# Halves at the ends of layers 2 and 3, and four column groups for two small products, in a four-layer graph network

## The chip, the cores and the metric

The kernel runs on one core of a Trainium2 chip. The metric is the device time of one launch in microseconds (us), from the first to the last instruction of the program. A core has a matrix engine (TensorE, "PE" in the profile, with "PEld" for its loads of the stationary operand), a vector engine (VectorE, "DVE"), a scalar engine (ScalarE, "ACT"), GpSimd ("POOL") and a queue engine that issues transfers (SyncE, "SP"). Each engine works through its own list of instructions in order and waits for the others by semaphores.

## The reference, cut to what matters

Sixteen graphs of 1024 nodes with 128 features pass through four layers. Each layer's output is added to its input and then normalised over the features.

```python
# x [16,1024,128], adj [16,1024,1024]
x = _layernorm(x + L0(x, adj))             # attention with one gate
x = _layernorm(x + L1(x, adj, nodemask))   # dilated adjacency, three SAGE steps, batch norm
x = _layernorm(x + L2(x, adj))             # attention with three gates
x = _layernorm(x + L3(x, adj))             # two graph convolutions

def _sage(x, adj, Wr, Wx, b, mf):          # three times in layer 1, with the dilated adj
    deg = jnp.clip(jnp.sum(adj, axis=-1, keepdims=True), 1.0, None)
    agg = jnp.einsum('bij,bjd->bid', adj, x) / deg
    out = agg @ Wr + x @ Wx + b
    ...

# the end of layer 2, with h_prime the attention's result
concat = jnp.concatenate([x, h_prime], axis=-1)
i_c = sigmoid(einsum('bnc,oc->bno', concat, ig_w) + ig_b)   # one number per node
f_c = sigmoid(einsum('bnc,oc->bno', concat, fg_w) + fg_b)
o_c = sigmoid(einsum('bnc,oc->bno', concat, og_w) + og_b)
h_joint = sigmoid(i_c * h_prime + f_c * x)
return o_c * tanh(h_joint)
```

## The kernel before

Sizes in the code: `P = 128`, `N = 1024`, `NT = N // P = 8`, `H2 = 2`, `B = 16`. The program runs layer 0, the dilation of the adjacency, the three steps of layer 1, and then layers 2 and 3 together. A layer's work on one batch is a generator, and `take_turns` lets several of them issue a stretch each in turn, so that the work of neighbouring batches lies side by side in the engines' lists.

Helpers. `halves` hands out a PSUM tile of 512 columns for each half of a batch, `turned` transposes a batch through it, `gates` (already used by layer 0) is the packed product that the change uses once more, and `normed` is a layer norm.

```python
    def gates(psum, out, *pairs):
        p = psum.tile([P, N // 4], F32, name="pq", tag="h")
        for i, (g, x) in enumerate(pairs):
            for q in range(4):
                nc.tensor.matmul(p[32 * q:32 * q + 32, :], g, x[:, q * N // 4:(q + 1) * N // 4], start=(i == 0),
                                 stop=(i == len(pairs) - 1), tile_position=(0, 32 * q))
        nc.scalar.copy(out, p)
        p = psum.tile([P, 2, P], F32, name="pg", tag="h")
        for t in range(2):
            nc.tensor.transpose(p[:, t, :], out[:, t * P:(t + 1) * P], identf)
        return p.rearrange("p t (q g) -> p q t g", q=4)

    def normed(small, r):
        st = small.tile([P, NT, 6], F32, name="ln_st")
        mv = small.tile([P, NT, 2], F32, name="ln_mv")
        for i in range(NT):
            nc.vector.bn_stats(st[:, i, :], r[:, i, :])
        for i in range(NT):
            nc.vector.bn_aggr(mv[:, i, :], st[:, i, :])
        rstd = power_mhalf(small, mv[:, :, 1], add=LN_EPS, name="ln_rstd")   # the power is on GpSimd
        nb = small.tile([P, NT], F32, name="ln_nb")
        nc.vector.scalar_tensor_tensor(nb, mv[:, :, 0], -1.0, rstd, op0=OP.mult, op1=OP.mult)
        for i in range(NT):
            nc.scalar.activation(r[:, i, :], r[:, i, :], AF.Identity, scale=rstd[:, i:i + 1], bias=nb[:, i:i + 1])
```

Layer 1, first step. `degree_product` multiplies the adjacency by a stationary block of twos, so that each of the 128 output rows holds the same row of degrees; the row then goes through memory to be turned and inverted.

```python
        def degree_product(A):
            for h in range(H2):
                c = slice(h * 512, (h + 1) * 512)
                acc = ps_a.tile([P, 512], F32, name="acc")
                for jt in range(NT):
                    nc.tensor.matmul(acc, twos[:, :P], A[:, jt, c], start=(jt == 0), stop=(jt == NT - 1))   # L1261
                yield acc, c
            # ... cut ...
            def first(self, b):
                st = self.batches[b]
                row = work.tile([1, N], F16, name="row", bufs=1)
                for acc, c in degree_product(st.A):
                    nc.scalar.copy(row[:, c], acc[0:1, :])                     # L1357
                d16 = small.tile([NT, P], F16, name="d16", bufs=1)
                nc.gpsimd.dma_start(d16, row)
                nc.vector.tensor_reduce(nodeg[:NT, b:b + 1], d16, AX.X, OP.min)  # L1360
                # ... cut: halve, clip, invert, store and load it as a broadcast tile rdeg ...
                # ... cut: transposes of x, the adjacency product, times rdeg ...
            def out(self, b):
                # ... cut: o = x @ Wx + ag @ Wr + b, by halves in PSUM tiles of the same pool ...
                for h, sq in enumerate(banks):
                    k = slice(4 * h, 4 * h + 4)
                    nc.scalar.activation(sq, o[:, k, :], AF.Square)
                    nc.vector.tensor_reduce(ss[:, k], sq, AX.X, OP.add)        # L1397
```

Layers 2 and 3. `before` makes layer 1's output, adds it to x, normalises and makes the attention's operands; `attention` is the eight-part attention; `after` has the gates, the mix, layer 2's norm, layer 3 and its norm.

```python
        def before(s, b):
            # ... cut: yT = layer 1's last product ...
            for p, c, k in turned(ps_h, yT):
                nc.vector.tensor_mul(yn[:, k, :], tiles3(p), half_rows(mf[:, b * NT + k.start:b * NT + k.stop]))
            nc.vector.tensor_add(s.xn, s.xn, yn)
            yield
            normed(small, s.xn)
            # ... cut: transposes of xn, hT, G, hn ...

        def after(s, b):
            hpT = wide("hpT")
            nc.scalar.activation(hpT, s.acc, AF.Relu)
            pg = ps_h.tile([P, NT, 3], F32, name="pg", tag="h")
            for i in range(NT):
                c = slice(i * P, (i + 1) * P)
                nc.tensor.matmul(pg[:, i, :], s.xT[:, c], gw[:, 0, :], start=True, stop=False)   # L1600
                nc.tensor.matmul(pg[:, i, :], hpT[:, c], gw[:, 1, :], start=False, stop=True)    # L1601
            # ... cut: bias, tanh, scale -> gt [P, NT, 3] ...
            for p, c, k in turned(ps_h, hpT):
                nc.vector.tensor_mul(yn[:, k, :], tiles3(p), half_rows(gt[:, k, 0]))
            f = rows("x3T")
            nc.vector.tensor_mul(f, s.xn, per_row(gt[:, :, 1]))
            nc.vector.tensor_add(yn, yn, f)
            nc.scalar.activation(yn, yn, AF.Tanh, scale=0.5)
            nc.scalar.activation(yn, yn, AF.Tanh, scale=0.5, bias=half)
            nc.vector.tensor_mul(yn, yn, per_row(gt[:, :, 2]))
            nc.vector.tensor_add(s.xn, s.xn, yn)
            yield
            normed(small, s.xn)
            # ... cut: layer 3 ...
            normed(small, s.xn)
            nc.gpsimd.dma_start(nat(out[b]), s.xn)
```

Of the kernel before, what the change touches and what calls it, by code (L numbers as in the profile page):

```python
# [9 lines left out]
F32 = mybir.dt.float32  # L10
# [629 lines left out]
def fast_kernel(ctx: ExitStack, tc: tile.TileContext, t: dict, out: bass.AP, flag: bass.AP):  # L640
# [142 lines left out]

        return v[:, :, None].to_broadcast([P, 4, P])

    def normed(small, r):

        st = small.tile([P, NT, 6], F32, name="ln_st")
        mv = small.tile([P, NT, 2], F32, name="ln_mv")
        for i in range(NT):  # L790
            nc.vector.bn_stats(st[:, i, :], r[:, i, :])  # L791
        for i in range(NT):
            nc.vector.bn_aggr(mv[:, i, :], st[:, i, :])
        rstd = power_mhalf(small, mv[:, :, 1], add=LN_EPS, name="ln_rstd")
        nb = small.tile([P, NT], F32, name="ln_nb")
        nc.vector.scalar_tensor_tensor(nb, mv[:, :, 0], -1.0, rstd, op0=OP.mult, op1=OP.mult)  # L796
        for i in range(NT):
            nc.scalar.activation(r[:, i, :], r[:, i, :], AF.Identity, scale=rstd[:, i:i + 1], bias=nb[:, i:i + 1])  # L798

    class Batch:  # L800
        pass
# [381 lines left out]
    class Layers23:  # L1183
# [53 lines left out]
    with ExitStack() as ph:  # L1237
# [16 lines left out]

        def degree_product(A):

            for h in range(H2):
                c = slice(h * 512, (h + 1) * 512)
                acc = ps_a.tile([P, 512], F32, name="acc")
                for jt in range(NT):  # L1260
                    nc.tensor.matmul(acc, twos[:, :P], A[:, jt, c], start=(jt == 0), stop=(jt == NT - 1))  # L1261
                yield acc, c

        def widened(A):

# [22 lines left out]
        class Step:  # L1288
# [63 lines left out]
            def first(self, b):  # L1352
# [7 lines left out]
                nc.vector.tensor_reduce(nodeg[:NT, b:b + 1], d16, AX.X, OP.min)  # L1360
# [116 lines left out]
    with ExitStack() as ph:  # L1477
# [54 lines left out]
        def before(s, b):  # L1532
# [60 lines left out]
        def after(s, b):  # L1593

            hpT = wide("hpT")
            nc.scalar.activation(hpT, s.acc, AF.Relu)
            pg = ps_h.tile([P, NT, 3], F32, name="pg", tag="h")
            for i in range(NT):
                c = slice(i * P, (i + 1) * P)
                nc.tensor.matmul(pg[:, i, :], s.xT[:, c], gw[:, 0, :], start=True, stop=False)  # L1600
                nc.tensor.matmul(pg[:, i, :], hpT[:, c], gw[:, 1, :], start=False, stop=True)  # L1601
            gt = small.tile([P, NT, 3], F32, name="gt")
            nc.vector.tensor_add(gt, pg, gb[:, None, :].to_broadcast([P, NT, 3]))
# [6 lines left out]
            nc.vector.tensor_mul(f, s.xn, per_row(gt[:, :, 1]))  # L1610
            nc.vector.tensor_add(yn, yn, f)
            nc.scalar.activation(yn, yn, AF.Tanh, scale=0.5)
            nc.scalar.activation(yn, yn, AF.Tanh, scale=0.5, bias=half)
            nc.vector.tensor_mul(yn, yn, per_row(gt[:, :, 2]))
            nc.vector.tensor_add(s.xn, s.xn, yn)
# [92 lines left out]
```

## Time and profile before

The median of three runs is 3050.43 us (3050.39 to 3054.73). Times below are from the profiled run, whose span is 3049.5 us and whose mean granted TensorE clock is 0.966.

| stretch, us from the start | what runs | length | PE busy | granted clock |
|---|---|---|---|---|
| 1145 to 1525 | layer 1, first step | 380.0 | 369.8 | 1.00 |
| 1780 to 1872 | end of layer 1, layers 2 and 3 begin | 92.0 | 64.7 | 0.88 |
| 1872 to 1957 | first batches of layers 2 and 3 | 85.0 | 82.0 | 0.93 |
| 1957 to 2936 | layers 2 and 3, batches side by side | 979.0 | 956.3 | 0.95 |
| 2936 to 3049.5 | the last two batches end | 113.5 | 78.3 | 0.84 |

A row of such a table is read from the view of busy time by stretch: PE busy is the time in which at least one matrix product was open, and the granted clock is the mean share of full speed that the throttle let through. Products overlap in the records, so the step from one start to the next, and not the length of a record, is what one of them costs. The profile page puts 58% of the chain that ended last on PE, and in its row of 40 slices (76 us each) PE stands at 9 in every slice from 1144 us on but three: the two from 1753 to 1906 us, where layer 1 gives way to layers 2 and 3, and the last one.

### The profile page before, as it was taken

How to read it: one execution, taken by the hardware profiler on the slowest of the kernel's cores; microseconds unless marked ns; L12 is line 12 of the kernel's file. 1: busy time of each engine (PE TensorE's matmuls, PEld its weight loads, DVE VectorE, ACT ScalarE, POOL GpSimd, SP SyncE). 2: the span in 40 equal slices, each digit the busy share in tenths (PEclk: the TensorE clock that was granted, in tenths of full speed). 3: DMA queues.
4: the chain of work that ended last, by engine and by line, in shares of the span. 5: the costliest groups of instructions: out<-in, count | busy, mean ns of one | idle time of the engine just before them, and what ended most of it. 6: DMA issues, size and time to landing. Idle time of an engine off the chain costs nothing.

```text
span 3049.5 us, 42855 instructions
## 1 busy us (share of the span) xinstructions
PE 2825.3 (93%) x15187; PEld 1794.2 (59%) x15250; DVE 2325.2 (76%) x5972; ACT 2018.8 (66%) x3425; POOL 315.2 (10%) x292
## 2 busy tenths in 40 slices
PE   7999999996999989999999987999999999999995
PEld 3444444443666657777788873556555555555554
DVE  7898889887999986666678785676766776777665
ACT  5877787773888886655555435666666666666653
POOL 0000000003000001111122231000000000000000
PEclk9999999997999999999999998999999999999997
DMA  5344344430000043223367692011112211111000
GB/s 162 131 159 152 132 138 159 152 118 29 2 2 2 2 158 107 88 91 120 122 231 251 227 336 76 35 63 59 66 57 71 73 57 56 56 56 56 21 14 22
DMA packets 123217, 297.97 MB, mean 98 GB/s; under 512 B 12656, under 2 KB 64624, under 8 KB 115824
## 3 DMA queue, kind: packets, MB, share of 16 engines
q1 hardware_dynamic: 102384, 211.13, 20.6%
q0 software_dynamic: 20608, 84.00, 7.7%
q8 instruction: 122, 2.00, 0.3%
q14 instruction: 103, 0.84, 0.1%
HBM read 211.04 MB, written 84.02 MB: 97 GB/s over the span
## 4 chain that ended last, share of the span: by engine, by line
PE 58%; DVE 21%; ACT 9%; DMA 5%; issue 5%; POOL 3%; SPq 0%; POOLq 0%; ACTq 0%; DVEq 0%
PE acc L1284 9%; PE pmm L723 8%; PE ph L1527 7%; PE acc L1590 6%; PE ph L765 6%; PE ph L758 4%; PE ph L1388 4%; DMA an<-in_adj 3%; ACT xn L798 3%; PE s L1131 2%; PE acc L969 2%; POOL ln_rstd L744 2%; PE ph L1513 2%; DVE mid L1085 2%; DVE ln_st L791 2%
## 5 line engine op out<-in xcount | busy, mean ns | idle before, releaser
L723 PE MATMUL pmm<-G,hT 128*128 128x512 f32 x1024 | 520.2, 630 | 1.9 <-DVE mx L1576 1.4
L723 PEld LDWEIGHTS pmm<-G,hT 128*128 128x128 f32 x1024 | 188.3, 201 | 174.2 <-issue 148.7
L798 ACT ACTIVATE xn<-xn,ln_nb,ln_rstd 128x128 f32<-128x128 f32 x512 | 206.6, 481 | 91.9 <-DVE ln_nb L796 91.9
L1590 PE MATMUL acc<-em,hs 128*128 128x512 f32 x512 | 256.0, 612 | 12.1 <-DVE hs L1587 10.5
L969 PE MATMUL acc<-em,hs 128*128 128x512 f32 x512 | 243.5, 599 | 18.2 <-DVE hs L966 16.8
L1284 PE MATMUL acc<-a,hi 128*128 128x512 f32 x768 | 242.0, 400 | 1.1 <-ACT hi L1251 0.9
L1284 PE MATMUL acc<-a,lo 128*128 128x512 f32 x768 | 241.2, 398 | 1.9 <-DVE lo L1252 1.9
L744 POOL TENSOR_TENSOR ln_rstd<-ln_rstd,mhalf 128x8 f32<-128x8 f32 x64 | 105.4, 1646 | 1324.2 <-DVE ln_rstd L741 1266.2
L1133 ACT ACTIVATE q<-s,negc 128x512 f16<-128x512 f32 x256 | 170.3, 696 | 58.2 <-DVE negc L1112 22.3
L915 ACT ACTIVATE ab<-an 128x1024 bf16<-128x1024 f32 x128 | 134.5, 1052 | 105.8 <-DMA an<-in_adj 66.6
L1131 PE MATMUL s<-step,carry 128*128 128x384 bf16 (+3 forms) x1034 | 197.6, 302 | 7.3 <-DVE carry L1101 3.2
L1576 DVE CUSTOM_DVE_ANT_0 em<-pmm,msk 128x1024 f32<-128x1024 f32 x128 | 156.0, 1219 | 54.7 <-PE pmm L723 51.9
L1145 ACT ACTIVATE carry<-pc,negone 128x512 fp8e4<-128x512 f32 x256 | 166.5, 698 | 35.7 <-PE pc L1144 26.3
L958 DVE CUSTOM_DVE_ANT_0 em<-pmm,msk 128x1024 f32<-128x1024 f32 x128 | 156.1, 1219 | 35.0 <-PE acc L969 30.5
L1571 ACT ACTIVATE msk<-A,nbig 128x1024 bf16<-128x1024 fp8e4 x128 | 146.0, 1141 | 50.2 <-DVE mx L1576 48.4
L1284 PEld LDWEIGHTS acc<-a,lo 128*128 128x128 f32 x768 | 142.9, 188 | 42.8 <-DVE lo L1252 9.5
L918 DVE SCALAR_TENSOR_TENSOR chk<-an 128x1024 fp8e4<-128x1024 f32 x128 | 156.3, 1221 | 14.0 <-DMA an<-in_adj 13.6
L1284 PEld LDWEIGHTS acc<-a,hi 128*128 128x128 f32 x768 | 141.7, 188 | 34.0 <-ACT hi L1251 1.4
L923 DVE TENSOR_SCALAR carry<-pt 128x1024 fp8e4<-128x1024 bf16 x128 | 155.7, 1217 | 6.2 <-PE pt L922 6.1
L969 PEld LDWEIGHTS acc<-em,hs 128*128 128x128 f32 x512 | 90.9, 190 | 113.9 <-issue 87.7
L1388 PE MATMUL ph<-Wx,hT 128*128 128x128 f32 x768 | 152.3, 281 | 4.9 <-DVE l2WT L709 3.2
L962 ACT ACTIVATE em<-em,nmx 128x1024 f32<-128x1024 f32 x128 | 146.9, 1147 | 12.3 <-DVE nmx L960 11.8
(285 smaller groups left out, 6448.6 us busy)
## 6 DMA issues: line engine op xcount, KB each, us to landing
an<-in_adj SPq DMA_DIRECT2D x128, 512.0 KB, 3.9
adj_d<-carry POOLq DMA_DIRECT2D x16, 1024.0 KB, 4.9
A<-dil_d SPq DMA_DIRECT2D x16, 1024.0 KB, 6.6
rdeg<-rdeg_d SPq DMA_DIRECT2D x32, 512.0 KB, 4.2
ag_d<-ag POOLq DMA_DIRECT2D x32, 512.0 KB, 5.5
ag<-ag_d SPq DMA_DIRECT2D x32, 512.0 KB, 6.3
A<-adj_d SPq DMA_DIRECT2D x16, 1024.0 KB, 4.8
xn<-in_x SPq DMA_DIRECT2D x16, 512.0 KB, 4.0
```

The lines of the kernel that those rows point to most:

```text
L723: nc.tensor.matmul(p[:, h * 512:(h + 1) * 512], lhsT, rhs[:, h * 512:(h + 1) * 512], start=True, stop=True)
L744: nc.gpsimd.tensor_tensor(r, r, mhalf[:, :n], op=OP.pow)
L765: nc.tensor.matmul(p, W, x[:, c], start=(i == 0), stop=(i == len(pairs) - 1))
L798: nc.scalar.activation(r[:, i, :], r[:, i, :], AF.Identity, scale=rstd[:, i:i + 1], bias=nb[:, i:i + 1])
L969: nc.tensor.matmul(s.acc[:, c], hs, em[:, c], start=(jt == 0), stop=(jt == NT - 1))
L1131: nc.tensor.matmul(s[:, lo or 0:], y, twos if lo is None else step[:, :512 - lo], start=(j == 0), stop=(j == len(terms) - 1))
L1133: nc.scalar.activation(q[:, h * 512:(h + 1) * 512], s, AF.Abs, bias=st.negc[:, i:i + 1])
L1145: nc.scalar.activation(Y[b][:, hb, ks], pc, AF.Relu, bias=negone, saturate=False)
L1284: nc.tensor.matmul(acc, part[:, jt, :], pieces[h * NT // 2 + i][:, j, :], start=(jt == 0 and p == 0), stop=(jt == NT - 1 and p == 1))
L1388: nc.tensor.matmul(p[:, i * P:(i + 1) * P], x[:, j * P:(j + 1) * P], W, start=(n == 0), stop=(n == 1))
L1527: nc.tensor.matmul(p, part[:, jt, :], A[:, jt, c], start=(jt == 0 and i == 0), stop=(jt == NT - 1 and i == 1))
L1590: nc.tensor.matmul(s.acc[:, c], hs, em[:, c], start=(jt == 0), stop=(jt == NT - 1))
```

## The change

Four things are done.

- Degrees of layer 1: instead of 16 products with 128 equal output rows on 512 columns, 32 products with 32 output rows on 256 columns, four of them in four column groups of the array. All sums of a batch fit one PSUM tile; the row is copied out in four pieces of 256 instead of two of 512.
- Gates of layer 2: the helper `gates` of layer 0 is used. The weights become the stationary operand, padded with zeros from 3 to 32 columns, and the nodes stream past it in four column groups; a copy on ScalarE and two transposes bring the result to the former layout.
- The first two batches: the sum in front of layer 1's norm, and the norm, are taken in two halves of four blocks.
- The last batch: the mix, layer 2's norm, layer 3's norm and the store of the output are taken in halves, and the store goes by SyncE's queue and not by GpSimd's.

```diff
-    def normed(small, r):
+    def normed(small, r, fine=False):
+        for k in spans(fine):
+            n = k.stop - k.start
+            # ... the same operations on blocks k.start .. k.stop, with tiles of their own ...
+    def spans(fine):
+        return [slice(0, NT // 2), slice(NT // 2, NT)] if fine else [slice(0, NT)]
...
-            self.gw = wts.tile([P, 2, 3], F32, name="l2gw")
+            self.gw = wts.tile([P, 2, 32], F32, name="l2gw")
+            nc.vector.memset(self.gw, 0.0)
...
         def degree_product(A):
-            for h in range(H2):
-                c = slice(h * 512, (h + 1) * 512)
-                acc = ps_a.tile([P, 512], F32, name="acc")
-                for jt in range(NT):
-                    nc.tensor.matmul(acc, twos[:, :P], A[:, jt, c], start=(jt == 0), stop=(jt == NT - 1))
-                yield acc, c
+            acc = ps_a.tile([P, 512], F32, name="acc")
+            for jt in range(NT):
+                for q in range(4):
+                    nc.tensor.matmul(acc[32 * q:32 * q + 32, :N // 4], twos[:, :32], A[:, jt, q * N // 4:(q + 1) * N // 4],
+                                     start=(jt == 0), stop=(jt == NT - 1), tile_position=(0, 32 * q))
+            for q in range(4):
+                yield acc[32 * q:32 * q + 1, :N // 4], slice(q * N // 4, (q + 1) * N // 4)
...
-                    nc.scalar.copy(row[:, c], acc[0:1, :])
+                    nc.scalar.copy(row[:, c], acc)
...
-            nc.vector.tensor_add(s.xn, s.xn, yn)
+            for k in spans(b < 2):
+                nc.vector.tensor_add(s.xn[:, k, :], s.xn[:, k, :], yn[:, k, :])
             yield
-            normed(small, s.xn)
+            normed(small, s.xn, b < 2)
...
-            pg = ps_h.tile([P, NT, 3], F32, name="pg", tag="h")
-            for i in range(NT):
-                c = slice(i * P, (i + 1) * P)
-                nc.tensor.matmul(pg[:, i, :], s.xT[:, c], gw[:, 0, :], start=True, stop=False)
-                nc.tensor.matmul(pg[:, i, :], hpT[:, c], gw[:, 1, :], start=False, stop=True)
+            pg = gates(ps_h, wide("x3T")[:, :N // 4], (gw[:, 0, :], s.xT), (gw[:, 1, :], hpT))
...
+            last = b == B - 1
+            for k in spans(last):
+                # ... mul, add, tanh, tanh, mul, add of the mix on blocks k ...
             yield
-            normed(small, s.xn)
+            normed(small, s.xn, last)
...
-            normed(small, s.xn)
-            nc.gpsimd.dma_start(nat(out[b]), s.xn)
+            normed(small, s.xn, last)
+            for k in spans(last):
+                (nc.sync if last else nc.gpsimd).dma_start(nat(out[b])[:, k, :], s.xn[:, k, :])
```

More of the change, by code (lines that the diff above doesn't have):

```diff
@@ L784, in half_rows @@
         return v[:, :, None].to_broadcast([P, 4, P])
-    def normed(small, r):
-        st = small.tile([P, NT, 6], F32, name="ln_st")
-        mv = small.tile([P, NT, 2], F32, name="ln_mv")
-        for i in range(NT):
[L791 to L798, printed above, removed]
+    def normed(small, r, fine=False):
+        for k in spans(fine):
+            n = k.stop - k.start
+            st = small.tile([P, NT, 6], F32, name="ln_st")
+            mv = small.tile([P, NT, 2], F32, name="ln_mv")
+            for i in range(n):
+                nc.vector.bn_stats(st[:, i, :], r[:, k.start + i, :])
+            for i in range(n):
+                nc.vector.bn_aggr(mv[:, i, :], st[:, i, :])
+            rstd = power_mhalf(small, mv[:, :n, 1], add=LN_EPS, name="ln_rstd")
+            nb = small.tile([P, NT], F32, name="ln_nb")
+            nc.vector.scalar_tensor_tensor(nb[:, :n], mv[:, :n, 0], -1.0, rstd, op0=OP.mult, op1=OP.mult)
+            for i in range(n):
+                nc.scalar.activation(r[:, k.start + i, :], r[:, k.start + i, :], AF.Identity,
+                                     scale=rstd[:, i:i + 1], bias=nb[:, i:i + 1])
+    def spans(fine):
+        return [slice(0, NT // 2), slice(NT // 2, NT)] if fine else [slice(0, NT)]
     class Batch:
@@ L1596, in after @@
             nc.scalar.activation(hpT, s.acc, AF.Relu)
-            pg = ps_h.tile([P, NT, 3], F32, name="pg", tag="h")
-            for i in range(NT):
-                c = slice(i * P, (i + 1) * P)
-                nc.tensor.matmul(pg[:, i, :], s.xT[:, c], gw[:, 0, :], start=True, stop=False)
-                nc.tensor.matmul(pg[:, i, :], hpT[:, c], gw[:, 1, :], start=False, stop=True)
+            pg = gates(ps_h, wide("x3T")[:, :N // 4], (gw[:, 0, :], s.xT), (gw[:, 1, :], hpT))
             gt = small.tile([P, NT, 3], F32, name="gt")
-            nc.vector.tensor_add(gt, pg, gb[:, None, :].to_broadcast([P, NT, 3]))
+            nc.vector.tensor_add(gt.rearrange("p (q t) g -> p q t g", t=2), pg[:, :, :, :3],
+                                 gb[:, None, None, :].to_broadcast([P, 4, 2, 3]))
             nc.scalar.activation(gt, gt, AF.Tanh, scale=0.5)
@@ L1609, in after, with gate @@
             f = rows("x3T")
[L1610 to L1615, printed above, removed]
+            last = b == B - 1
+            for k in spans(last):
+                def gate(g):
+                    return gt[:, k, g][:, :, None].to_broadcast([P, k.stop - k.start, P])
+                y, x = yn[:, k, :], s.xn[:, k, :]
+                nc.vector.tensor_mul(f[:, k, :], x, gate(1))
+                nc.vector.tensor_add(y, y, f[:, k, :])
+                nc.scalar.activation(y, y, AF.Tanh, scale=0.5)
+                nc.scalar.activation(y, y, AF.Tanh, scale=0.5, bias=half)
+                nc.vector.tensor_mul(y, y, gate(2))
+                nc.vector.tensor_add(x, x, y)
             yield
-            normed(small, s.xn)
+            normed(small, s.xn, last)
             diag = bass.AP(tensor=s.A8.tensor, offset=s.A8.offset, ap=[list(s.A8.ap[0]), [N + P, NT], [1, P]])
```

## The prediction

> **What bounds the kernel now.** I read the page first, for the engine that carries the span.
>
> ```profile
> PE 2825.3 (93%) x15187; PEld 1794.2 (59%) x15250; DVE 2325.2 (76%) x5972; ACT 2018.8 (66%) x3425; POOL 315.2 (10%) x292
> ...
> PE 58%; DVE 21%; ACT 9%; DMA 5%; issue 5%; POOL 3%; SPq 0%; POOLq 0%; ACTq 0%; DVEq 0%
> ```
>
> PE is busy for 93% of the span and holds 58% of the chain that ended last. An average hides stages, so next comes the view of busy time by stretch: one batch of layer 1's first step in its first half, one in its second half, and one batch of layers 2 and 3. After the stretch and its length come PE, PEld, DVE, ACT and POOL busy, then the granted clock.
>
> ```profile
> 1254.78:1278.77 23.99, 23.99 (x129) 18.65 (x129) 16.62 (x28) 14.38 (x19) 3.83 (x6) 1.00 0.26 88
> ...
> 1427.97:1453.76 25.79, 24.17 (x130) 18.67 (x129) 16.50 (x28) 14.50 (x19) 3.84 (x6) 1.00 0.36 123
> ...
> 2172.45:2244.40 71.95, 70.22 (x265) 42.08 (x265) 50.05 (x155) 48.08 (x94) 5.85 (x4) 0.95 0.17 59
> ```
>
> In all three PE has next to no gap while DVE and ACT have a third of their time free. So a product removed from PE here is worth its step, from its start to the next start. In the second row PE stands still for 1.6 us. The third row has a clock of 0.95, not 1.00. Both matter below.
>
> The timeline of PE gives the steps. First the degrees, then layer 0's gates, which already run in four column groups:
>
> ```profile
> 1443.87 2.76 PE L1261 MATMUL acc<-A,step 128*128 128x512 fp8e4 x12
> 1446.46 0.39 PE L1388 MATMUL ph<-Wx,hT 128*128 128x128 f32 x2
> ```
>
> ```profile
> 83.73 0.59 PE L723 MATMUL pmm<-G,hT 128*128 128x512 f32 x1
> ...
> 84.49 0.40 PE L774 MATMUL pq<-hpT,l0gw 128*32 128x256 f32 x4
> 84.82 0.70 PE L723 MATMUL pmm<-G,hT 128*128 128x512 f32 x1
> ```
>
> Twelve degree products take 1446.46 - 1443.87 = 2.59 us, 0.216 each. Layer 0's four float32 products are eight records (two passes each); they start at 84.25, the second four at 84.49, and the next work at 84.82. A round of four thus takes 0.24 us.
>
> Then layer 2's gates, and the same place in stretches of 3.41 us with the clock:
>
> ```profile
> 2200.07 1.02 PE L723 MATMUL pmm<-G,hT 128*128 128x512 f32 x2
> 2200.93 0.28 PE L1600 MATMUL pg<-l2gw,xT 128*128 128x3 f32 x2
> ...
> 2204.42 1.09 PE L758 MATMUL ph<-identf,hpT 128*128 128x128 f32 x4
> 2205.31 3.14 PE L723 MATMUL pmm<-G,hT 128*128 128x512 f32 x4
> ```
>
> ```profile
> 2201.02:2204.43 3.41, 3.41 (x34) 3.41 (x32) 2.19 (x17) 1.63 (x2) 0.00 (x0) 1.00 0.18 41
> 2204.43:2207.84 3.41, 3.41 (x9) 1.88 (x9) 0.84 (x3) 0.22 (x1) 1.64 (x1) 0.50 0.65 271
> 2207.84:2211.25 3.41, 3.41 (x12) 1.72 (x11) 3.41 (x9) 2.73 (x7) 0.00 (x0) 1.00 0.00 0
> ```
>
> The gates hold PE for 2204.42 - 2200.93 = 3.49 us: 32 records, each with three columns and a full 128x128 load, 0.11 a step. Right behind them the clock is 0.50 for 3.41 us. The two 512-column passes ahead take 0.86 us, 0.43 each; after them (2205.31) four take 3.14. A half-clock stretch costs 1.7 us of PE.
>
> [...] records without a gap, but with three columns each, are not enough to keep the clock. [...] From 83.73 to 84.82 are 1.09 us; less 0.43 for the first pass and 0.48 for two rounds, 0.18 us remain for going in and out. [...] a copy of 1x512 took 574 ns here and one of 128x256 took 357.
>
> **Part 1, degrees.** Before: 16 x 0.216 = 3.46 us a batch. After: 32 products are eight rounds. A float32 round is 0.24 us against 0.215 of streaming (half of 0.43), so it adds 0.025; an fp8 round should be 0.108 + 0.025 = 0.133, eight make 1.06. In the built program they stand in two stretches, 20 and 12, so twice 0.18 is added: 1.42. Saved 2.04 a batch, and as PE is full, 16 x 2.04 = 33 us.
>
> The wait of 1.6 us in the second half of the batches has a cause that the change touches:
>
> ```profile
> 1451.58 0.27 DVE L1360 TENSOR_REDUCE nodeg<-d 8x1 f32<-8x128 f16 x1 [2.44 <-DMA d<-row]
> ...
> 1452.69 0.52 PE L758 MATMUL ph<-identf,n 128*128 128x128 f32 x3 [1.62 <-issue]
> ```
>
> VectorE waits 2.44 us for the row of degrees to come back from its transfer, and behind that instruction stands the reduction (L1397, 1451.92) that frees the PSUM tile PE needs for its transposes. In the built program that reduction stands ahead of the row. I expect 1.2 of the 1.6 back on seven or eight batches: 9 us. Against it, four copies of the row at about 0.36 make 1.44 us after the last product, where one of 0.57 was left before, so the row leaves 0.9 us later. The broadcast degrees landed about 1459.4 and were first used at 1466.6, so 7 us of slack cover it.
>
> **Part 2, gates.** After: two pairs of two passes are four rounds, 0.96 + 0.18 = 1.14, and two transposes at 0.11: 1.36 us against 3.49. Saved 2.1 a batch; for the 14 batches of the loop 30 us. Second, the clock: 979 us at 0.95 mean near 98 us at half speed, two stretches a batch, one of them behind the gates (the other at 2228, behind waits for the norm). With the three-column products gone I expect one stretch less a batch, 14 x 1.7 = 24 us. Against it, the ScalarE copy between the gates and their transposes. In the built program it stands behind three casts of A (1.0 us each) that start when hpT is done, while PE has only 0.86 us of other work in between: a new wait of about 0.8 us, and perhaps some more where the mix and the norm now wait: minus 12 in all. The loop gives 42.
>
> **Part 3, halves.** They touch only the ends, where PE idles (113.5 us with 78.3 busy at the end). In the last batch the mix runs from 2975.2 to 2985.1; two tanh of 1.06 and 1.15 can lie beside VectorE's half: 2 us. Two norms, each about 1.64 + 0.63 + 1.65 + 3.2 in series, can let the first half's 1.6 us of ScalarE go ahead: 1.5 each, 3 in all, less than half of the length as the power on GpSimd is now paid twice. The store in two transfers: 1. The first two batches: 2. The gates at the two ends: 4. Together 12.
>
> Sum: 33 + 9 + 42 + 12 = 96; 3050 - 96 = 2954 us.
>
> **Rivals.** (a) A new wait takes the gates' place. For it: the copy sits in ScalarE's list behind 3 us of casts, and the list is fixed. If PE waits 2 us there, [...] the half clock stays, and the loop gives nothing: 3050 - 54 = 2996. Against it: the products of five attention parts are built in behind, and ScalarE has 24 us of a batch free. (b) VectorE and ScalarE become the bound in the loop: layer 3 is a chain of products and elementwise work, and with less attention left beside it PE would wait at each link. That gives half of the loop's gain, 2975. (c) Packed fp8 products do not overlap as the float32 ones do, since each needs its own load; [...] degrees give 14 us and not 33: 2973. Against it, layer 0's loads and products of a round do overlap. (d) The clock recovers wholly, both stretches a batch: 2930.
>
> **Range and chances.** Degrees are near certain for 25 to 45 us with the wait; the loop may give 0 to 75; the ends 4 to 15. The combinations run from 2915 to 3000. The line of 2% below 3050 is 2989. Only (a) together with a weak degree part ends above it, so faster by over 2%: 0.83; within 2%: 0.16; slower: 0.01, as nothing added costs more than it removes on PE.
>
> **What would show it.** Right: a first-half batch of layer 1's first step in 22.0 us, a second-half one below 22.6; stretches of 20 and 12 degree records taking some 0.8 and 0.6; gates with transposes spread over less than 2.5 us of PE; the loop's clock at 0.97 or more, and its period near 69 us, from 72. Wrong: PE waiting for ScalarE's copy by more than 1.5 us a batch, a clock still at 0.95 in the loop, or a wait for the row of degrees in layer 1.

## The result and the profile after

The changed kernel takes 3008.07 us (3006.44 to 3009.76) against 3050.41 us for the kernel before (3049.17 to 3054.73): a ratio of 0.9859, 95% interval 0.9842 to 0.9876. The gain is 42 us where 96 were predicted, and 3008 lies above the range that ended at 3000.

The page of the changed kernel, in the two lines that were shown of before: busy time of the engines, and their shares of the chain that ended last.

```profile
PE 2738.6 (91%) x15219; PEld 1719.6 (57%) x15282; DVE 2329.1 (77%) x5987; ACT 2028.3 (67%) x3475; POOL 324.1 (11%) x295
...
PE 36%; DVE 23%; issue 21%; ACT 9%; DMA 6%; POOL 5%; SPq 0%; POOLq 0%; DVEq 0%; ACTq 0%
```

PE lost 86.7 us of busy time, near the 91 that four terms of the prediction take from PE (33, 30, 24 and 4), but the span lost only 42. So half of what was taken from PE came back as waiting. The shares of the chain say less about it: PE falls from 58% to 36%, but "issue", time for which the profile shows no wait, rises from 5% to 21%. The view by stretch says where the waiting is. The rows are the same three stages as before (columns: stretch, length, PE, PEld, DVE, ACT and POOL busy, granted clock, DMA share, GB/s).

```profile
1244.01:1266.04 22.03, 21.84 (x145) 17.83 (x144) 16.49 (x27) 14.69 (x21) 3.83 (x5) 1.00 0.27 96
1394.21:1418.65 24.44, 21.91 (x145) 17.93 (x144) 16.49 (x28) 14.80 (x21) 3.84 (x5) 1.00 0.37 130
2177.93:2248.75 70.82, 65.66 (x250) 37.82 (x249) 50.61 (x155) 48.31 (x95) 6.82 (x4) 0.98 0.17 60
```

The first half of layer 1's first step went from 23.99 to 22.03 us, as predicted. In the row of the second half PE has 2.3 us less to do and stands still for 2.5 us instead of 1.6, so 25.79 became 24.44. Not all of the second half waits: in both kernels it is the last six batches of the sixteen. In the changed kernel the batches before them take 22.0 us each, and these 24.2 to 24.3, one of them 26.0 with 3.4 us at a granted clock of 0.50, from about 1421.2 on. In the two rows of the loop PE has 4.6 us less to do, and the batch takes 1.1 us less. In the mean of the loop's 13 batches, from one `hpT` to the next, PE has 3.5 us less to do (70.1 to 66.7) and the batch takes 1.1 us less (71.9 to 70.8). Over the loop as a whole, before and after:

```profile
1957.90:2936.00 978.10, 955.42 (x3612) 578.62 (x3611) 678.98 (x2084) 651.68 (x1261) 78.68 (x54) 0.95 0.17 55
1936.00:2860.00 924.00, 869.83 (x3262) 500.14 (x3261) 659.16 (x2015) 631.78 (x1233) 81.95 (x52) 0.98 0.16 57
```

PE stands for 22.7 us of the first and for 54.2 us of the second.

The timeline of PE in the second half shows what PE stands before; the number in brackets is the idle time and what ended it.

```profile
1416.50 0.63 PE L1293 MATMUL acc<-a,hi 128*128 128x512 f32 x2
1418.65 0.73 PE L1268 MATMUL acc<-A,step 128*32 128x256 fp8e4 x20 [1.52 <-DVE ag L1432]
```

The twenty degree records come out as estimated, but they wait 1.52 us for a PSUM accumulator, which VectorE's product with the degrees (L1432) frees. The other 1.0 us that PE stands in this row is a wait for `lo`, which VectorE makes too (L1260). VectorE and the queues in the same batch:

```profile
1406.56 0.69 DVE L1406 TENSOR_REDUCE ss<-ph 128x4 f32<-128x512 f32 x1 [0.67 <-ACT ph L1405]
1407.17 0.68 DVE L1399 TENSOR_TENSOR o<-ph,b 128x512 f32<-128x512 f32 x1
1410.44 0.27 DVE L1369 TENSOR_REDUCE nodeg<-d 8x1 f32<-8x128 f16 x1 [2.59 <-DMA d<-row]
...
1417.91 0.68 DVE L1432 TENSOR_TENSOR ag<-acc,rdeg 128x512 f32<-128x512 f32 x1
```

```profile
1405.27 0.32 SPq L1340 DMA_DIRECT2D A<-dil_d  x1
```

```profile
1405.58 0.51 POOL L1368 DMA_DIRECT2D d<-row  x1 [7.60 <-ACT row L1366]
```

The reduction of the squares (L1406) now stands ahead of the row's minimum (L1369), as the prediction had read from the built program. VectorE still stands 2.59 us before that minimum, and the freeing of the accumulator is behind it. The row is 2 KB and was issued at 1405.58, 0.3 us behind a load of 1 MB.

The first batch of the step loses more, and to the same list:

```profile
1152.45 0.28 DVE L1369 TENSOR_REDUCE nodeg<-d 8x1 f32<-8x128 f16 x1 [7.57 <-DMA d<-row]
...
1154.97 1.22 PE L1293 MATMUL acc<-a,lo 128*128 128x512 f32 x2 [4.67 <-DVE lo L1260]
```

Here VectorE's `lo`, which the adjacency product needs, stands behind the minimum. With 3.32 us more for ScalarE's `hi`, which comes behind the four copies of the row, PE stands 8.0 us. In the kernel before, `lo` stood ahead of the minimum, and PE stood 0.7 us at this place.

In the loop, the gates themselves:

```profile
2177.93 0.64 PE L774 MATMUL pq<-xT,l2gw 128*32 128x256 f32 x8
2178.39 0.61 PE L774 MATMUL pq<-hpT,l2gw 128*32 128x256 f32 x8
2178.93 1.12 PE L723 MATMUL pmm<-G,hT 128*128 128x512 f32 x2
2179.89 0.43 PE L779 MATMUL pg<-identf,x3T 128*128 128x128 f32 x2
2180.16 0.60 PE L758 MATMUL ph<-identf,hpT 128*128 128x128 f32 x4
```

From start to next start the gates take 1.00 us and their transposes 0.27, 1.27 together where 3.49 were and 1.36 were expected. The transposes carry no bracket: PE does not wait for ScalarE's copy. What PE does wait for in this batch is in the view of waits (total, times, longest, in us):

```profile
PE ph L758 <- ACT xn L800: 2.2, 1, 2.2
PE ph L1522 <- DVE ehi L1509: 1.6, 1, 1.6
```

The first is for the scaled rows of layer 2's norm (`xn`), at 2205.01, and the second for an operand of layer 3 (`ehi`) behind it. Over the 13 batches the two make 42 of the 54 us that PE waits. ScalarE's timeline in the first microseconds of that batch:

```profile
2175.73 1.00 ACT L1607 ACTIVATE hpT<-acc 128x1024 f32<-128x1024 f32 x1
2176.64 2.92 ACT L1641 CAST A<-A 128x1024 fp32r<-128x1024 fp8e4 x3
...
2181.27 1.15 ACT L1582 ACTIVATE msk<-A,nbig 128x1024 bf16<-128x1024 fp8e4 x1 [1.44 <-DVE mx L1587]
...
2183.34 3.19 ACT L800 ACTIVATE xn<-xn,ln_nb,ln_rstd 128x128 f32<-128x128 f32 x8 [0.82 <-DVE ln_nb L798]
2186.43 0.21 ACT L1612 ACTIVATE gt<-gt 128x24 f32<-128x24 f32 x1
```

The gates' tanh (L1612, 0.21 us) starts 9.7 us after `hpT` is done. It stands behind the eight norm scalings of layer 3 of the batch before (L800, 3.19 us), which in turn wait for GpSimd's power (1.64 us from 2181.47). Behind the tanh come the mix of this batch and its layer 2 norm, for whose rows PE waits. In the kernel before the same tanh stood ahead of the mask and of the scalings, 4.0 us after `hpT`:

```profile
2199.76 1.01 ACT L1596 ACTIVATE hpT<-acc 128x1024 f32<-128x1024 f32 x1
2200.67 1.98 ACT L1626 CAST A<-A 128x1024 fp32r<-128x1024 fp8e4 x2
2204.81 0.22 ACT L1604 ACTIVATE gt<-gt 128x24 f32<-128x24 f32 x1 [2.16 <-DVE gt L1603]
2208.53 1.15 ACT L1571 ACTIVATE msk<-A,nbig 128x1024 bf16<-128x1024 fp8e4 x1 [3.49 <-DVE mx L1576]
...
2209.67 3.17 ACT L798 ACTIVATE xn<-xn,ln_nb,ln_rstd 128x128 f32<-128x128 f32 x8
```

The mix was not earlier by as much. In the kernel before, VectorE's next step with the gates (L1605) stood behind the norm's last small operation (`ln_nb`), so the first product of the mix began 7.9 us after `hpT`, against 10.1 in the batch above (in the mean of the loop 8.1 and 9.7).

Nothing in the change's source asks for this order. That the list came out so because the packed gates pass through one more copy is a guess, which no run tests.

My theory after the result: two lists decide it. In layer 1, VectorE's list holds an instruction that waits for the small row behind the large load. In the loop, ScalarE's list holds the tanh behind the scalings. The rival: the terms were mis-sized in themselves (degrees 19 us and not 33, gates some 15 and not 46), and neither order matters.

### The profile page after: what moved, and what is told of

The parts are those of the page before. It is cut to its first block, busy times and chain, and to the rows that moved or that the text cites. A ratio compares the mean times of both kernels' runs of the same rounds, so it can differ in the third digit from the quotient of the medians.

```text
span 3007.9 us, 42998 instructions
## 1 busy us (share of the span) xinstructions
PE 2738.6 (91%) x15219; PEld 1719.6 (57%) x15282; DVE 2329.1 (77%) x5987; ACT 2028.3 (67%) x3475; POOL 324.1 (11%) x295
## 4 chain that ended last, share of the span: by engine, by line
PE 36%; DVE 23%; issue 21%; ACT 9%; DMA 6%; POOL 5%; SPq 0%; POOLq 0%; DVEq 0%; ACTq 0%
PE ph L1536 8%; PE acc L1293 6%; PE ph L765 5%; PE acc L1601 4%; DMA an<-in_adj 4%; PE pmm L723 3%; POOL ln_rstd L744 3%; DVE ln_st L793 3%; ACT xn L800 3%; PE ph L1397 3%; PE ph L758 3%; PE ph L1522 2%; DVE em L1587 2%; ACT em L969 2%; PE acc L976 2%
## 5 line engine op out<-in xcount | busy, mean ns | idle before, releaser
L723 PE MATMUL pmm<-G,hT 128*128 128x512 f32 x1024 | 505.9, 611 | 7.7 <-DVE mx L1587 7.2
L800 ACT ACTIVATE xn<-xn,ln_nb,ln_rstd 128x128 f32<-128x128 f32 x512 | 207.6, 481 | 115.2 <-DVE ln_nb L798 115.2
L723 PEld LDWEIGHTS pmm<-G,hT 128*128 128x128 f32 x1024 | 178.5, 193 | 175.5 <-issue 139.9
L976 PE MATMUL acc<-em,hs 128*128 128x512 f32 x512 | 243.3, 598 | 16.7 <-DVE hs L973 15.2
L744 POOL TENSOR_TENSOR ln_rstd<-ln_rstd,mhalf 128x8 f32<-128x8 f32 (+1 forms) x68 | 113.6, 1671 | 1329.1 <-DVE ln_rstd L741 608.8
L1601 PE MATMUL acc<-em,hs 128*128 128x512 f32 x512 | 249.3, 606 | 3.6 <-DVE hs L1598 1.9
L1140 ACT ACTIVATE q<-s,negc 128x512 f16<-128x512 f32 x256 | 170.5, 697 | 57.9 <-DVE negc L1119 22.3
```

Of the source, the lines that this page charges most:

```text
L723: nc.tensor.matmul(p[:, h * 512:(h + 1) * 512], lhsT, rhs[:, h * 512:(h + 1) * 512], start=True, stop=True)
L744: nc.gpsimd.tensor_tensor(r, r, mhalf[:, :n], op=OP.pow)
L800: nc.scalar.activation(r[:, k.start + i, :], r[:, k.start + i, :], AF.Identity, scale=rstd[:, i:i + 1], bias=nb[:, i:i + 1])
L976: nc.tensor.matmul(s.acc[:, c], hs, em[:, c], start=(jt == 0), stop=(jt == NT - 1))
L1140: nc.scalar.activation(q[:, h * 512:(h + 1) * 512], s, AF.Abs, bias=st.negc[:, i:i + 1])
L1601: nc.tensor.matmul(s.acc[:, c], hs, em[:, c], start=(jt == 0), stop=(jt == NT - 1))
```

## The experiments

All ratios are against the kernel before on the same chip; a gain is 1 less the ratio, times 3048 us.

**One part alone.** Three kernels take the kernel before and one part of the change each.

```diff
 deg_only:    + column groups in degree_product, row copied from four slices
 gates_only:  + pg = gates(...), gw padded to 32 columns
 halves_only: + spans(...) in mix, norms and last store
```

> The kernel before with the column groups of the degrees alone; gates, halves and the order of the first two batches stay as before. The prediction's sum gives this part 33 us (the degree products) plus 9 us (the wait it brings back on 7 or 8 batches in part): about 2998 to 3010 us. Rival, read from the trace of the changed kernel, where only the first 8 batches of layer 1 got shorter by the 2 us each: 17 to 25 us, so 3025 to 3033 us. In its trace the period of the first 8 batches should be near 22.0 us, and of the second 8 above 24 us by the rival, below 22.6 us by the prediction.

> The kernel before with the packed gates of layer 2 alone. The prediction gives this part 42 us in the loop and 4 us at its ends, so about 3004 us, whichever other part stands beside it. If the norm chain of layers 2 and 3 ends last, as the changed kernel's trace suggests (TensorE busy 4 us less in a batch, waiting 3 us more), 12 to 18 us: 3032 to 3038 us, with a period of 71 us, single half-clock stretches and a wait of about 2 us at the first product behind the norm of layer 3. If this kernel gains more than 25 us, the longer chain is not the gates' own doing but comes from the halves.

> The kernel before with the halves of mix and norms for the first two and last batches, and the last store on one queue; degrees and gates as before. The prediction's sum has mix 2, norms 3, store 1 and first two batches 2: 8 us, so 3042 us. If the three parts add up to the 42 us measured, and the other two have their rivals' values, 3 to 8 us. A slower kernel here would say that the halves spoil the order of the loop.

| kernel | us | ratio, 95% interval | gain |
|---|---|---|---|
| degrees alone | 3028.20 | 0.9938 (0.9918 to 0.9957) | 19 |
| gates alone | 3033.86 | 0.9945 (0.9925 to 0.9966) | 17 |
| halves alone | 3042.60 | 0.9987 (0.9973 to 1.0000) | 4 |
| all (the change) | 3008.07 | 0.9859 (0.9842 to 0.9876) | 43 |

The three add up to 40, so the parts do not spoil each other: each fell short by itself, against 33 + 9, 42 + 4 and 8 predicted. In the trace of the gates alone the tanh comes 8.8 to 9.7 us after `hpT`, as with all parts, and in that of the halves alone 4.0 to 4.9, as before.

**The tanh ahead of the scalings.** Layer 3's last scaling and its store are put in a list and issued behind the next batch's tanh.

```diff
             nc.scalar.activation(gt, gt, AF.Tanh, scale=0.5)
+            while pending:
+                pending.pop(0)()
...
-            normed(small, s.xn, last)
-            ... store ...
+            normed(small, s.xn, last, later)     # scalings into `pending`,
+            later.append(store)                  # except for the last two batches
```

> The changed kernel, with the norm scaling and the store of layer 3 of a batch issued behind the gates' tanh of the next batch instead of ahead of it (the last two batches as they were). Theory one, the gates' tanh stands in ScalarE's list behind eight scalings that wait for GpSimd's power, and the chain from the mixed rows to the norm is 3 us longer by that: TensorE's waits for xn and ehi (2.2 and 1.6 us of a batch) go, period 71 to 68 us, 2970 to 2980 us. Theory two, the chain is held elsewhere (the packed gates' add with its broadcast, GpSimd's power, VectorE's list): tanh comes 3 us earlier, but the next thing waits in its place, and the time stays within 10 us of 3008.

Measured: 2982.65 us, ratio 0.9788 (0.9768 to 0.9808). The gain is 65 us, 22 more than the change alone. ScalarE, with the same first microseconds of a batch:

```profile
2170.17 1.02 ACT L1615 ACTIVATE hpT<-acc 128x1024 f32<-128x1024 f32 x1
...
2176.01 0.21 ACT L1620 ACTIVATE gt<-gt 128x24 f32<-128x24 f32 x1
2176.93 3.19 ACT L801 ACTIVATE xn<-xn,ln_nb,ln_rstd 128x128 f32<-128x128 f32 x8 [0.71 <-DVE ln_nb L798]
```

The tanh is at 4.7 to 4.8 us after `hpT` in each batch of the loop, and two whole batches of the loop, by stretch, are

```profile
1970.01:2038.62 68.61, 65.97 (x252) 37.67 (x251) 50.30 (x154) 48.11 (x97) 6.00 (x5) 0.98 0.18 63
2176.01:2244.72 68.71, 64.53 (x252) 36.94 (x251) 50.27 (x154) 48.07 (x97) 6.09 (x5) 1.00 0.18 61
```

The wait for `xn` is gone and that for `ehi` falls from 25 us over 13 batches to 1, and the period falls from 70.8 to 68.7. Theory one holds for these waits and the period, though 2983 is a little above its 2970 to 2980. In seven of thirteen such batches the clock is 1.00, in six 0.98, and the two rows take the same time: half speed costs PE 1.5 us of busy time there and the batch nothing. So the loop is now bound by its chain, and PE's waits are for other links of it (here over 68.6 us):

```profile
PE acc L1607 <- DVE hs L1604: 2.4, 2, 2.3
PE pmm L723 <- DVE mx L1593: 1.7, 1, 1.7
```

How long the chain is, the last small operation of layer 2's norm (`ln_nb`) tells. In the batches shown above it starts 24.6 us behind the end of `hpT` (2200.77) in the kernel before, 27.5 (2176.73) in the changed kernel and 22.3 (2171.19) with the deferral:

```profile
2225.32 0.17 DVE L796 SCALAR_TENSOR_TENSOR ln_nb<-ln_mv,ln_rstd 128x8 f32<-128x8 f32 x1 [1.25 <-POOL ln_rstd L744]
```

```profile
2204.26 0.17 DVE L798 SCALAR_TENSOR_TENSOR ln_nb<-ln_mv,ln_rstd 128x8 f32<-128x8 f32 x1 [1.55 <-POOL ln_rstd L744]
```

```profile
2193.50 0.17 DVE L798 SCALAR_TENSOR_TENSOR ln_nb<-ln_mv,ln_rstd 128x8 f32<-128x8 f32 x1 [1.25 <-POOL ln_rstd L744]
```

The same deferral with the gates alone, without degrees and halves:

> The kernel before with the packed gates and the deferred scaling of layer 3, without degrees and halves. The packed gates alone gave 14 us of the 46 predicted. If the gates' tanh behind the scalings was what ate the rest, this kernel gains 38 to 46 us: 3002 to 3010 us, loop period 68.7 us as with all parts. If the deferred scaling gains by itself something that has nothing to do with the gates, the period would still be near 71 us without the halves, and the gain 15 to 25 us.

Measured: 3010.76 us, ratio 0.9867 (0.9848 to 0.9885). The gain is 41 us where the gates alone gave 17. The period is 68.7, and the prediction's 46 for this part is nearly there. The deferral was not run on the kernel before alone. PE stands there for only 1.7 us in a batch of the loop, so it could bring back some 24 us at most by shorter waits (an estimate, 14 times 1.7).

**The row behind the load, tried by trace order.** The first two kernels moved a piece of source: the minimum and reciprocal of the degrees to one turn later, or the load of the packed adjacency to one turn later. Two more combine them with the deferral above.

```diff
 late_nodeg (in first):         late_load (in load, l == 0):
+ yield                         + x load first
+ hT transposes                 + yield
+ yield                           A8 load
  minimum, scale, reciprocal
```

> The changed kernel with the four VectorE operations behind the row of degrees (minimum, scaling, reciprocal, and the store behind them) traced one turn later, behind the transposes of the rows that step turns. Theory one, that VectorE, standing 2.6 us before the row of degrees, holds up all behind it and so the accumulator of the next batch: the wait of the first operation falls under 1 us, the second 8 batches of layer 1 go from 24.4 to near 22.2 us, 8 times 2.2 or about 17 us, 2991 us. Theory two, the accumulator is late for another reason (the row's own transfer, the normalization's chain behind GpSimd): within 5 us of 3008.

> The changed kernel with the 1 MB load of the batch's packed adjacency in the first step of layer 1 issued one turn later, so that it is not just ahead of the row's small transfer. If that load makes the row slow, the row lands 1.5 to 2 us after its issue instead of 4 to 5, VectorE's wait of 2.6 us goes, and the second 8 batches reach about 22.2 us: 2991 us. If the transfer is slow by itself, the wait stays near 2.6 us and the time within 5 us of 3008; if the load itself is now late, the kernel is slower than 3012 us and the wait for the adjacency shows it.

> The changed kernel with both the deferred norm scaling of layer 3 (alone 2983 us) and the degree chain traced one turn later. They act in different stages, so if both theories hold the gains add: 2983 less 17 is 2966 us. If the degree chain is not the cause in layer 1, 2980 to 2985 us.

> The version before it with the late load as well. If either of the two (later chain, later load) takes the whole wait away, the second adds nothing: 2966 us, within 4 us. If each takes a part, up to 8 us less than the kernel with the chain alone; if the load is late for its product, more.

Measured: 3012.99 (0.9885; 0.9864 to 0.9905), 3008.02 (0.9871; 0.9839 to 0.9903), 2986.22 (0.9789; 0.9764 to 0.9815) and 2984.24 us (0.9782; 0.9759 to 0.9804). No gain, but the traces say that nothing was tested. With the later chain:

```profile
1410.68 0.68 DVE L1399 TENSOR_TENSOR o<-ph,b 128x512 f32<-128x512 f32 x1
1413.96 0.27 DVE L1374 TENSOR_REDUCE nodeg<-d 8x1 f32<-8x128 f16 x1 [2.60 <-DMA d<-row]
```

and with the later load:

```profile
1405.21 0.32 SPq L1344 DMA_DIRECT2D A<-dil_d  x1
```

The minimum stands where it stood, and the load goes out at the same moment, as it waits for its buffer: the view of waits has the load behind the last cast of an earlier batch (`SPq L1340 <- DVE a L1280`, in the changed kernel: 61.2 us in six waits). The source moved and the lists did not.

**The same two, with the order held.** Now an ordering edge (`issue_after`) holds the chain behind the floor of the row norms on VectorE, or the load behind that of the degrees' reciprocals on the queue.

```diff
 nodeg_behind:                                   load_behind:
+with issue_after(floor of rn):                  +with issue_after(load of rdeg):
+    minimum, scale, reciprocal                  +    load of A8
```

> The changed kernel with the chain behind the row of degrees (minimum, scaling, reciprocal) held in VectorE's list until behind the floor of the row norms, where VectorE waits 1.8 us for GpSimd's power anyhow. The earlier kernel with this aim (traced one turn later) left VectorE's list in that order, so it tested nothing. If VectorE's wait for the row holds the accumulator, the wait of 2.6 us goes and the second 8 batches of layer 1 fall from 24.4 to near 22.3 us: 2991 us. If not, 3003 to 3013 us, with a wait of TensorE for the accumulator that stays near 1.5 us.

> The changed kernel with the 1 MB load of layer 1's first step held in the queue's list until behind the load of the degrees' reciprocals. The earlier kernel with this aim moved the load in the source, but the load waits for its buffer and went out at the same moment. If the load makes the row's small transfer slow, the row lands 1.5 to 2 us after its issue instead of 4.8, VectorE's wait goes, and the second 8 batches take near 22.3 us: 2991 us. If the row is slow without it, the wait stays and so does the time, 3003 to 3013 us.

> Deferred norm scaling of layer 3 (alone 2983 us) with the degree chain held behind the floor. If both act, 2966 us; if the chain in layer 1 is not what holds the accumulator, 2979 to 2986 us.

Measured: the held chain 3008.78 us (0.9854; 0.9832 to 0.9876), the held load 2998.13 (0.9822; 0.9803 to 0.9841), the held chain with the deferral 2975.60 (0.9749; 0.9731 to 0.9767). With the held load, VectorE, GpSimd and the queue:

```profile
1403.14 0.69 DVE L1412 TENSOR_REDUCE ss<-ph 128x4 f32<-128x512 f32 x1
1403.75 0.27 DVE L1375 TENSOR_REDUCE nodeg<-d 8x1 f32<-8x128 f16 x1
```

```profile
1401.85 0.51 POOL L1374 DMA_DIRECT2D d<-row  x1 [7.60 <-ACT row L1372]
```

```profile
1407.84 0.32 SPq L1364 DMA_DIRECT2D rdeg<-rdeg_d  x1
1408.20 0.43 SPq L1349 DMA_DIRECT2D A<-dil_d  x1
```

```profile
1398.77:1420.47 21.70, 21.70 (x146) 18.04 (x144) 16.51 (x27) 14.84 (x21) 3.83 (x5) 1.00 0.39 146
```

The minimum starts 1.9 us after the row's issue and waits for nothing, and a batch of the second half takes 21.70 us with PE full. It is even shorter than the 22.03 of the first half in the changed kernel. The 32 degree records now stand in one stretch, 0.99 us from its start to the next product (1398.93 to 1399.92); in that first half they stand in two, of 0.92 (0.19 of it a wait for `lo`) and 0.44. Only in the last batch does a load again go out 0.3 us ahead of the row; there the row takes 4.7 us once more, and VectorE waits 2.8. The held chain also ends the wait, but its instructions now stand in a place that all batches pay for:

```profile
1256.00:1278.40 22.40, 21.85 (x147) 17.84 (x146) 16.52 (x28) 14.69 (x21) 3.83 (x5) 1.00 0.26 95
1413.00:1435.40 22.40, 21.85 (x147) 17.84 (x145) 16.51 (x28) 14.70 (x20) 3.83 (x5) 1.00 0.41 142
```

These batches take 2.0 us less in the second half and 0.4 more in the first. From the first row of degrees to the last, the traces give 325.8 us against 331.8 in the changed kernel, 6 us less. Alone the held chain can't be told from the change, and the 2991 us expected were missed; with the deferral it brings 12 us more than the deferral alone, of which its trace bears out 6. So the time does not settle it, but the waits do, and the cause of the wait in the last six batches is shown twice over: take the load away from before the row, or VectorE's list away from behind it, and the wait goes.

**Do the causes add up, and whose are they?** Three kernels of the edits above: the change with the deferral and the held load; the kernel before with degrees and held load; the kernel before with the held load alone.

> The changed kernel with the deferred norm scaling (alone 2983 us, 25 less than the changed kernel) and the load held behind the reciprocals of degrees (alone 2998 us, 10 less). They act in different stages: if the two lost terms are independent the gains add, 2970 to 2975 us. Had the earlier stage's gain only been noise, 2980 to 2985 us. The prediction of 2954 us would be met in mechanism but for what is then left: about 16 to 20 us.

> The kernel before with the column groups of the degrees and the held load, without gates and halves. The prediction gives the degrees 33 us and the wait of the second half 9 us, 42 us in all: 3010 us. The degrees alone gave 19 us. If the 1 MB load is what ate the rest, 30 to 42 us (3010 to 3022); if the degrees' gain was mis-sized in itself, 19 to 25 us (3027 to 3033).

> The kernel before with nothing but the held load. Degrees and held load together gave 41 us, degrees alone 20, so the load is worth 21 us beside the column groups. If the load only gives back what the column groups ran into, it is worth here no more than the 1.6 us of wait in seven batches, 11 us, or less: 3037 to 3048 us. If it is worth 18 us or more here too (3030 us), it is a gain of its own that has nothing to do with the change, and the degrees' term was too large by itself.

| kernel | us | ratio, 95% interval | gain |
|---|---|---|---|
| change, deferral, held load | 2968.74 | 0.9739 (0.9714 to 0.9764) | 80 |
| degrees, held load | 3007.34 | 0.9864 (0.9839 to 0.9889) | 41 |
| held load alone | 3037.24 | 0.9968 (0.9957 to 0.9979) | 10 |

The held load is worth 10 us in the kernel before, the degrees alone 19, and both together 41. So the degrees are worth 31 us where the row is not held up (23 to 39 by the two intervals; by the traces 27, as the time from the first row to the last falls from 340.9 to 314.0), and about 12 were eaten by waits. The first of the three kernels has the lowest time of all, though not clear of the 2975.60 above.

## Why the prediction was wrong, step by step

- **Degrees, 33.** Right for a batch: one of the first half lost 1.96 us against 2.04 expected, so the rival of mis-sized degrees falls. The step "as PE is full, 16 x 2.04" failed for the first batch of the step, where PE is not full: there it stands 8.0 us and not 0.7, so 7 us are lost.
- **The wait of 1.6 us, 9 of it back.** This step failed: "In the built program that reduction stands ahead of the row. I expect 1.2 of the 1.6 back." The order was read rightly, but the wait was taken to belong to one instruction. It belongs to VectorE's list, which still stands 2.6 us before the row, and PE meets the next thing that list frees, the accumulator. With PE's own work 2.3 us shorter, it stands 2.5 us instead of 1.6. The "seven or eight batches" were misread too: six batches of the kernel before have the wait. Over these six PE stands 14.0 us and not 9.3, and 1.7 more go to the stretch at a clock of 0.50 (an estimate, half of its 3.4 us), so not 9 us came back, but some 6 were lost. Together: 33 less 7 less 6 is 20, and 19 were measured for the degrees alone.
- **The row, 0.9 us later.** It leaves 1.5 us later (2.4 us behind the last degree product, from 0.9). The slack of 7 us was counted for the broadcast degrees, which is the last use of the row. The first use, VectorE's minimum, had none.
- **Gates and clock, 30 + 24.** Right. 1.27 us for 3.49, and one half-speed stretch less in a batch: over the loop the clock went from 0.95 to 0.98, and the time at 0.50 from 89 us of 978 to 44 of 924, near 26 stretches of 3.41 us before and 13 after. PE's work fell by 3.5 us a batch, 49 in 14.
- **New waits, "minus 12 in all".** This is the step that failed most, by a term of its sum that was mis-sized. The copy was feared, and PE did not wait for it. PE's waiting in the loop went from 22.7 us in 978 to 54.2 in 924, that is from 1.7 to 4.2 us in a batch; times 14 this rise is 35 us and not 12. 54 less 35 is 19, near the 17 measured. With the gates alone the deferral gained about 24. By PE's own account only 10 of these are shorter waits (4.1 to 3.4 us a batch); the rest shows as less busy time at a higher clock (0.99 for 0.98).
- **What stood behind it.** From the end of `hpT` to the norm's last small operation (`ln_nb`) it took 25.2 us in the mean of the loop's batches before, 25.6 after (by turns 23.9 and 27.5) and 22.3 with the deferral. The chain had hardly grown. PE's work beside it had become 3.5 us shorter, and so the chain ended last. This is rival (b), in its effect; what it missed is that the same work on VectorE and ScalarE makes a chain 3.3 us shorter in another order. How much of that is the tanh's own place is not separated: the deferral brings the tanh forward by 4.0 to 4.9 us, the mix's first product by 2.3 to 3.2, and with it no power on GpSimd takes more than 1.87 us in the loop, where six took 2.62 (see the last section).
- **Halves, 8 beside the gates' 4.** Measured 4 (0 to 8). In its trace the stretch from the last `hpT` to the end is 3.3 us shorter (88.5 to 85.2), where 6 were expected, so 8 looks too large; the times alone leave it open.
- **Rivals.** (a) fell: no wait for the copy, and the clock recovered. (c) fell: 32 packed degree products take 1.06 us in one stretch, as estimated, where they stand so. (d) came true in part, and only with the deferral: about half of the loop's batches (seven of thirteen) keep a clock of 1.00, but as the chain bounds them by then, it gains nothing.
- **The range.** The parts' own lower ends, 25, 0 and 4, add up to 29 and reach 3021 us, not 3000. And (a) at 2996 lies above 2989 by itself, without a weak degree part. The range was narrower than its terms, and the 0.83 for more than 2% too high.

With both causes removed 80 us are gained (72 to 87), not 96. The gates with the deferral lack 5 of their 46, 2 of them perhaps in the last batch (from `hpT` to the end 81.8 us in the change, 84.1 with the deferral), and the halves 4. That degrees and held load reach 41, near the 42 predicted, is in part luck: 10 of these come from an edit that the prediction did not have. The rest is within the intervals and stays open.

## What to carry to other kernels

A product taken from a full engine is worth its time only until the next chain ends last (in the loop 3.5 us less of PE's work in a batch gave 1.1); before counting it, measure that chain's length against the engine's new busy time, stage by stage. When an edit changes what the compiler lists, read the order of the other engines around it: a short instruction behind a long group that waits passes part of that wait on to all that needs it (here the tanh came 4.0 to 4.9 us later, and the mix 2.3 to 3.2). And an experiment that moves source has moved nothing until the list or the trace shows it.

## What the runs showed of the hardware

**A small transfer behind a large one.** The same 2 KB row lands 1.5 us after its issue, or 4.8 when it goes out 0.3 us behind a load of 1 MB, although the row goes through GpSimd's queue and the load through SyncE's. Of the row's transfers in the changed kernel:

```profile
DMA to landing us min/median/max: 1.5/1.6/4.8
```

Issued 0.3 us after the load, the row was there at 1410.4; the load itself took 4.8 us from 1405.27. In the kernel before, the row went out 1.0 us after the load and took 3.9 to 4.0 us: there too it landed 0.2 us after the load. With the load held back, the wait is gone (see the experiments). Why the row lands no earlier than the load, no run shows; other sizes were not tried.

**GpSimd's power beside a VectorE addition.** In the changed kernel the power took 1.64 us, but 2.62 once in every second batch of the loop:

```profile
2201.61 2.62 POOL L744 TENSOR_TENSOR ln_rstd<-ln_rstd,mhalf 128x8 f32<-128x8 f32 x1 [13.86 <-DVE sm L1594]
```

```profile
2201.49 1.22 DVE L1554 TENSOR_TENSOR xn<-xn,yn 128x1024 f32<-128x1024 f32 x1
```

VectorE's addition began 0.12 us earlier and ran on until 2202.71. All six slow powers of the loop begin 0.12 or 0.13 us behind this addition. In the seven other batches the same power takes 1.66 us, and the addition starts only when it is over (2272.57, for a power from 2270.66). The 0.98 us that the power took longer are near the 1.1 us that the addition had still to go. That the addition causes it is an inference from this, as no run moves the addition alone. With the deferral the power is never above 1.87 us in the loop; how much of the 22 us is due to that was not separated. The 0.98 us in six of 13 batches is some 6 us, an estimate of its direct part.

**Half clock behind a wait, but not behind each.** Two stretches of the changed kernel's loop:

```profile
2202.80:2206.20 3.40, 1.04 (x5) 0.46 (x4) 1.94 (x14) 1.74 (x5) 1.42 (x1) 1.00 0.00 0
2206.22:2209.63 3.41, 3.41 (x8) 1.97 (x9) 2.85 (x17) 3.11 (x8) 1.64 (x1) 0.50 0.02 5
```

PE was busy for 1.04 us of the first, in the wait for the norm, and the next ran at a clock of 0.50. Busy time alone does not decide it: PE was busy for 2.59 of the 3.41 us ahead of the half-speed stretch at 2134.54, and for only 1.73 of the 3.41 us from 2059.45, which a clock of 1.00 followed. What does decide it, these runs do not show. Where PE sets the end, such a stretch costs up to 1.7 us on top of the wait ahead of it (an estimate, half of 3.41 us). With the deferral, where PE does not set the end, it cost nothing: 68.61 us at 0.98 against 68.71 at 1.00.
